# Expert blocks ordered by first token group, half of the final sums moved into the block loop, and smaller loads in the first attention layer

## The chip, the cores and the metric

The kernel runs as one program on one core of a Trainium2 chip. The metric is device time in microseconds (us) of one execution. The engines are named as the profile names them: PE (TensorE, with PEld for its weight loads), DVE (VectorE), ACT (ScalarE), POOL (GpSimd) and SP (SyncE); a "q" behind a name (SPq, POOLq) is the engine's instruction queue, from which DMAs are issued.

## The reference, cut to what matters

There are 32 batches of 112 rows with 256 features. Each of four branches normalises `x`, computes something and adds it to `x` under a gate:

```
x = x + tanh(g0) * attention_16_heads_of_16(norm(x), ctx)     # layer 0, 375 context rows per batch
x = x + tanh(g1) * gated_recurrence_over_32_batches(norm(x))
x = x + tanh(g2) * attention_16_heads_of_64(norm(x), ctx)     # layer 1
x = x + tanh(g3) * (shared_expert(norm(x)) + routed)          # 64 experts, 8 per row
aff = xf @ centroids.T;  idx = top_k(aff + bias, 8)
w = sigmoid(aff at idx), normalised over the 8
h = silu(xf @ W_up[e]);  routed[row] = sum over its 8 experts of w * (h @ W_down[e])
```

So 3584 rows go to 8 experts each, which makes 28672 pairs of a row and an expert.

## The kernel before

Layer 0 walks over 128 steps `n` (batch `b = n // 4`, four heads each). Keys come from PE and ACT, and eight small DMAs on the SP queue (L432, `kT<-k`) spread 16 heads over partitions; the queries of a group of four batches are spread by 16 more on the same queue (L416, `qp<-q`). `inputs(g)` (L359 to L368) loads `x`, the context and recurrence weights of a whole group from POOL's queue. PE, DVE and ACT follow the order as written; POOL does not, and is placed by the scheduler. Then come the recurrence and layer 1, in which `route(b)` picks the experts of batch `b` and, eight times per batch, POOL's indirect DMA (L286) scatters the 112 normalised rows with their weights into `xrows`, a table in HBM with a region for each expert. Rows stand there in order of batch.

The experts follow. Tables (L967 to L1032) are built from the counts per expert. The blocks of 128 rows come in two parts: the first 256 rows of each expert, as 64 steps `n < E` of two blocks, and then 136 single blocks, two a step, whose expert and place are found in the tables at run time. `run(lo, hi)` is the block loop; its PE, DVE, ACT and SP order is the written one. At step `n` it does, in this order:

- `rows_in(n+4)`: SP loads the rows of step n+4 (L1042; or, for `n >= E`, two register loads from `x_at`, L1048, and two DMAs, L1049). `xblk` has 5 buffers. Every eighth step up to 40, `weights` adds 2 MB of expert weights on SP.
- `turned(n)`: PE transposes (L1057), ACT copies (L1059), and DVE finds each row's weight and target (`own`, `dst32`, L1062 to L1072).
- `up(n-2)`: PE (L1085 or L1095), ACT (L1101), DVE (L1102).
- `down(n-4)`, or for `n >= E` `hidden_turned(n-4)` (L1109, L1111) and `down(n-6)`: PE (L1118), one half of `yblk` scaled by ACT (L1122) and the other by DVE (L1125), and two indirect DMAs by POOL (L1129) that scatter the two blocks into `yrows`, which has one place for each of the 28672 pairs. `yblk` has 4 buffers.

A second `run` for blocks past 136 stands under `tc.If(found > NSURE)`. At the end, 32 sums each load the 8 results of a batch's 112 rows, 896 KB, from `yrows` (L1176), add them up (L1179, L1180 on POOL, L1185), add the sum to `x` (L1186) and store each pair of batches (L1188).

Of the kernel before, what the change touches and what calls it, by code (L numbers as in the profile page):

```python
# [43 lines left out]
G = 4  # L44
# [8 lines left out]
SBLK = 2 * E  # L53
NSURE = 136
# [15 lines left out]
def flamingo_kernel(ctx: ExitStack, tc: tile.TileContext, a: dict, out: bass.AP):  # L70
# [34 lines left out]
    nc.vector.tensor_copy(e_col, e_col32)  # L105
    place32 = const.tile([S, TOPK], I32, tag="place32", name="place32")
    nc.gpsimd.iota(place32, [[1, TOPK]], base=0, channel_multiplier=B * TOPK)
# [4 lines left out]
    nc.vector.memset(seen[:, 0, :], 0.0)  # L112
    half = const.tile([S, G], F32, tag="half", name="half")
# [76 lines left out]
    def route(b, pool, psum):  # L190
# [16 lines left out]
            row[:, P_DST : P_DST + TOPK], place, float(b * TOPK), None, ALU.add  # L207
# [39 lines left out]
        po = psum.tile([S, D + E], F32, tag="mm", name=f"pos_{b}")  # L247

        pr = po[:, D:]
        nc.tensor.matmul(pr, earlier16, chosen, start=True, stop=False)  # L250
        nc.tensor.matmul(pr, ones16[:, :S], before, start=False, stop=True)
        nc.tensor.matmul(po[:, :D], hs, sdn, start=True, stop=True)
        nc.vector.reciprocal(w, w)
# [41 lines left out]
    with ExitStack() as att:  # L295
# [14 lines left out]
        with ExitStack() as ph:  # L310
# [48 lines left out]
            def inputs(g):  # L359
                nc.gpsimd.dma_start(  # L360
                    xs[g], a["x"][g * G : (g + 1) * G].rearrange("b s d -> s b d")
                )
                nc.gpsimd.dma_start(cts[g], a["ctxT"][:, g * G : (g + 1) * G, :])


                if 2 <= g < 6:
                    w, name = ((wg, "wg"), (ug, "ug"), (wot, "wot"), (uot, "uot"))[g - 2]
                    nc.gpsimd.dma_start(w, a[name].rearrange("(c p) m -> p c m", p=128))  # L368
# [35 lines left out]
            def queries0(g, i):  # L404

                pq = ps_m.tile([128, GT], F32, tag="mm", name=f"pq0_{g}_{i}")
                for k in range(2):
                    nc.tensor.matmul(
                        pq, wq[:, k, 128 * i : 128 * i + 128], xTs[g][:, k, :],
                        start=(k == 0), stop=(k == 1),  # L410
                    )

                q = kvp.tile([128, GT], F32, tag="q", name=f"q0_{g}_{i}")
                nc.scalar.activation(q, pq, AF.Identity, bias=bq4[:, i : i + 1], scale=0.25)
                for h in range(8):
                    nc.sync.dma_start(  # L416
                        qps[g % 2][h % 4 * 32 : h % 4 * 32 + 16, 2 * i + h // 4, :],
                        q[16 * h : 16 * h + 16, :],
                    )
# [120 lines left out]
            def output0(b):  # L540
# [10 lines left out]
                nc.tensor.engine, nc.vector.engine, nc.scalar.engine,  # L551
# [9 lines left out]
            for i in range(2):  # L561
                queries0(0, i)
# [3 lines left out]
            for n in range(4 * B + 7):  # L566
                b, g = n // 4, n % 4
                ng, turn = b // G + 1, (b % G, g)
                if ng < NG and turn == (0, 0):
                    inputs(ng)  # L570
# [27 lines left out]
                if ng < NG and turn in ((3, 1), (3, 2)):  # L598
                    queries0(ng, g - 1)
# [359 lines left out]

    w_at = wp.tile([1, NBLK], I32, tag="w_at", name="w_at")  # L960
    x_at = wp.tile([1, NBLK], I32, tag="x_at", name="x_at")
    n_blk = wp.tile([1, 1], I32, tag="n_blk", name="n_blk")
    first = wp.tile([128, SBLK + NBLK], F32, tag="first", name="first")
    nowhere = wp.tile([128, SBLK + NBLK], F32, tag="nowhere", name="nowhere")
    own = wp.tile([128, SBLK + NBLK, 2], F32, tag="own", name="own")
    dst32 = wp.tile([128, SBLK + NBLK], I32, tag="dst32", name="dst32")
    total = seen[:, B % G, :]  # L967
    with tc.tile_pool(name="tables", bufs=1) as ep:
        pc = ps_x.tile([E, 1], F32, tag="x", name="pc_n")
        nc.tensor.matmul(pc, total, ones16[:, 0:1], start=True, stop=True)  # L970
        n_e = ep.tile([E, 1], F32, tag="n_e", name="n_e")
        nc.vector.tensor_copy(n_e, pc)
# [6 lines left out]
        above = ep.tile([E, NT // 128 - 2], F32, tag="above", name="above")  # L979
        nc.vector.tensor_scalar(above, steps[:E, 2 : NT // 128], n_e, None, ALU.is_lt)  # L980
        blocks = ep.tile([E, 1], F32, tag="blocks", name="blocks")
        nc.vector.tensor_reduce(blocks, above, AX.X, ALU.add)
        pb = ps_x.tile([E, 1], F32, tag="x", name="pb_before")
        nc.tensor.matmul(pb, earlier[:E, :E], blocks, start=True, stop=True)
        pt = ps_x.tile([1, 1], F32, tag="x", name="pt_blocks")
        nc.tensor.matmul(pt, blocks, ones[:E, 0:1], start=True, stop=True)
        nc.vector.tensor_copy(n_blk, pt)
        before = ep.tile([E, 2], F32, tag="before", name="before")
        nc.vector.tensor_copy(before[:, 0:1], pb)
        nc.vector.tensor_tensor(before[:, 1:2], before[:, 0:1], blocks, ALU.add)  # L990

        nc.vector.tensor_scalar(before, before, 128.0, None, ALU.mult)
        is_e = ep.tile([E, NBLK], F32, tag="is_e", name="is_e")
        past = ep.tile([E, NBLK], F32, tag="past", name="past")
        nc.vector.tensor_scalar(is_e, steps[:E, :NBLK], before[:, 0:1], None, ALU.is_ge)
        nc.vector.tensor_scalar(past, steps[:E, :NBLK], before[:, 1:2], None, ALU.is_ge)
        nc.vector.tensor_tensor(is_e, is_e, past, ALU.subtract)
# [4 lines left out]
        nc.vector.tensor_copy(base[:, 2:3], before[:, 0:1])  # L1002
        nc.vector.tensor_copy(base[:, 3:4], n_e)
        of = []
        for i in range(4):
            wide = ep.tile([E, 128], F32, tag=f"wide{i}", name=f"wide_{i}")
            nc.vector.tensor_scalar(wide, ones[:E], base[:, i : i + 1], None, ALU.mult)
            pg = ps_x.tile([128, NBLK], F32, tag="x", name=f"pg_{i}")
            nc.tensor.matmul(pg, wide, is_e, start=True, stop=True)
            if i == 0:  # L1010
                nc.vector.tensor_copy(w_at, pg[0:1, :])
            else:
                t = ep.tile([128, NBLK], F32, tag=f"of{i}", name=f"of_{i}")
                nc.vector.tensor_copy(t, pg)
                of.append(t)
        region, start, n_of = of
        nc.vector.tensor_tensor(start, steps[:, 2:], start, ALU.subtract)
# [19 lines left out]
    live = {}  # L1037

    def rows_in(n):
        x = ep.tile([128, 2, PW], F32, tag="xblk", name=f"xblk_{n}", bufs=5)  # L1040
        if n < E:
            nc.sync.dma_start(  # L1042
                x, xrows[n * NT : n * NT + 256, :].rearrange("(i p) c -> p i c", p=128)
            )
        else:
            for i in range(2):
                e = 2 * n + i - SBLK
                at = nc.sync.value_load(x_at[0:1, e : e + 1], min_val=0, max_val=E * NT - 128)  # L1048
                nc.sync.dma_start(x[:, i, :], xrows[bass.ds(at, 128), :])  # L1049
        live[n] = [x]  # L1050

    def turned(n):
        x = live[n][0]
        px = ps_x.tile([128, 2, 2, 128], F32, tag="x", name=f"px_{n}")
        for i in range(2):
# [15 lines left out]
        nc.vector.tensor_reduce(own[:, 2 * n : 2 * n + 2, :], both, AX.X, ALU.add)  # L1071
        nc.vector.tensor_tensor(  # L1072
            dst32[:, 2 * n : 2 * n + 2], own[:, 2 * n : 2 * n + 2, 1],
            nowhere[:, 2 * n : 2 * n + 2], ALU.max,
        )
        live[n] = [xT]

# [36 lines left out]
    def down(n):  # L1114
        hT, ats = live.pop(n)
        py = ps_y.tile([128, 2, D], F32, tag="y", name=f"py_{n}")
        for i in range(2):
# [3 lines left out]
        y = ep.tile([128, 2, D], F32, tag="yblk", name=f"yblk_{n}", bufs=4)  # L1121
        nc.scalar.activation(  # L1122
            y[:, 0, :], py[:, 0, :], AF.Copy, scale=own[:, 2 * n, 0:1]
        )
        nc.vector.tensor_scalar(  # L1125
            y[:, 1, :], py[:, 1, :], own[:, 2 * n + 1, 0:1], None, ALU.mult
        )
        for i in range(2):
            disjoint("yrows", nc.gpsimd.indirect_dma_start(  # L1129
                out=yrows[:, :],  # L1130
                out_offset=bass.IndirectOffsetOnAxis(
                    ap=dst32[:, 2 * n + i : 2 * n + i + 1], axis=0
# [3 lines left out]
            ))  # L1136

    def run(lo, hi):
        with tc.manual_schedule(engines={
            nc.tensor.engine, nc.vector.engine, nc.scalar.engine, nc.sync.engine,  # L1140
        }):
            for n in range(lo, min(lo + 4, hi)):
                rows_in(n)
            for n in range(lo, hi + 6):
                if n + 4 < hi:
                    rows_in(n + 4)
# [11 lines left out]
                if lo <= n - 6 < hi and E <= n - 6:  # L1158
                    down(n - 6)

    sure = (SBLK + NSURE) // 2
    run(0, sure)
# [6 lines left out]
    ep = ctx.enter_context(tc.tile_pool(name="sum", bufs=4))  # L1169
    ys = {}  # L1170
    with tc.manual_schedule(engines={nc.vector.engine}):
        for b in range(B + 1):
            if b < B:

                y = ep.tile([S, TOPK, 2 * D], F32, tag="y8", name=f"y8_{b}")[:, :, :D]
                nc.sync.dma_start(  # L1176
                    y, yrows.rearrange("(p b k) d -> b p k d", b=B, k=TOPK)[b]
                )
                nc.vector.tensor_tensor(y[:, 0:4], y[:, 0:4], y[:, 4:8], ALU.add)  # L1179
                nc.gpsimd.tensor_tensor(y[:, 0:2], y[:, 0:2], y[:, 2:4], ALU.add)  # L1180
                ys[b] = y
            if b > 0:
                c = b - 1
                y, xb = ys.pop(c), xs[c // G][:, c % G, :]
                nc.vector.tensor_tensor(y[:, 0], y[:, 0], y[:, 1], ALU.add)  # L1185
                nc.vector.scalar_tensor_tensor(xb, y[:, 0], tg[:, 3:4], xb, ALU.mult, ALU.add)  # L1186
                if c % 2 == 1:
                    nc.scalar.dma_start(  # L1188
                        out[c - 1 : c + 1].rearrange("b s d -> s b d"),
                        xs[c // G][:, c % G - 1 : c % G + 1, :],  # L1190
                    )
# [57 lines left out]
```

## Time and profile before

| What | Value |
|---|---|
| Median of 6 runs | 2524.71 us (2517.46 to 2530.61) |
| Profiled execution, its own time | 2525.33 us |
| Its span, first to last instruction | 2523.5 us |
| Mean granted TensorE clock | 0.954 |
| PE busy, share of the span | 90% |
| DVE busy | 66% |
| POOL busy | 34% |
| Layer 0 / recurrence / layer 1 | about 27 to 580 / to 805 / 828 to 2015 us |
| Expert tables and blocks | about 2024 to 2396 us |
| Final sums | 2398.7 to 2523.5 us |

The page divides the span into 40 slices of 63 us and gives for each engine the busy share in tenths. A group of instructions is written "line engine operation out<-in xcount | busy us, mean ns of one | idle us of the engine before them <-what ended the idle time". In the timeline each row is start, duration, engine, line and operation, with the idle time before it in brackets. In the list of waits a row is "who waited <- for whom: us in total, times, longest".

### The profile page before, as it was taken

How to read it: one execution, taken by the hardware profiler on the slowest of the kernel's cores; microseconds unless marked ns; L12 is line 12 of the kernel's file. 1: busy time of each engine (PE TensorE's matmuls, PEld its weight loads, DVE VectorE, ACT ScalarE, POOL GpSimd, SP SyncE). 2: the span in 40 equal slices, each digit the busy share in tenths (PEclk: the TensorE clock that was granted, in tenths of full speed). 3: DMA queues.
4: the chain of work that ended last, by engine and by line, in shares of the span. 5: the costliest groups of instructions: out<-in, count | busy, mean ns of one | idle time of the engine just before them, and what ended most of it. 6: DMA issues, size and time to landing. Idle time of an engine off the chain costs nothing.

```text
span 2523.5 us, 55527 instructions
## 1 busy us (share of the span) xinstructions
PE 2278.0 (90%) x20058; PEld 1793.8 (71%) x20058; DVE 1672.1 (66%) x4933; ACT 1169.2 (46%) x3088; POOL 854.9 (34%) x1014
## 2 busy tenths in 40 slices
PE   6999999999998999999999999999999969999700
PEld 3777777777997777777777777777777657789600
DVE  4666666666335677777777777777777755577577
ACT  1555444443333555555555555555555435455300
POOL 4111111010000024343334334433333457777733
PEclk7999999999999999999999999999999979999955
DMA  8111111112800000000000000000000189876499
GB/s 232 31 31 30 29 29 31 31 30 88 268 1 1 1 5 29 29 29 27 27 29 28 28 27 29 29 29 29 25 29 29 39 294 314 249 200 197 122 274 250
DMA packets 142536, 203.87 MB, mean 81 GB/s; under 512 B 24983, under 2 KB 119785, under 8 KB 142256
## 3 DMA queue, kind: packets, MB, share of 16 engines
q1 hardware_dynamic: 104384, 103.25, 15.3%
q0 software_dynamic: 31536, 90.82, 10.8%
q10 hardware_dynamic: 6336, 6.16, 0.8%
q8 instruction: 164, 2.69, 0.5%
q14 instruction: 116, 0.95, 0.1%
HBM read 100.67 MB, written 88.74 MB: 75 GB/s over the span
## 4 chain that ended last, share of the span: by engine, by line
PE 52%; DMA 7%; DVE 4%; ACT 2%; issue 2%; POOL 1%; SPq 0%; POOLq 0%; ACTq 0%; DVEq 0%
PE ps_a L810 7%; PE pv L788 7%; PE pk L773 7%; PE pav L860 7%; PE po_a L875 5%; PE pt_a L839 5%; PE pq L760 4%; DMA y<-yrows 3%; PE py L1118 3%; DMA yrows<-yblk,dst 3%; PE ph L1095 2%; PE px L1057 1%; ACT kT L777 1%; DMA xblk<-xrows 1%; POOL yrows L1129 1%
## 5 line engine op out<-in xcount | busy, mean ns | idle before, releaser
L286 POOL DMA_INDIRECT xrows<-row,at x256 | 257.0, 1004 | 521.7 <-DVE at L283 329.1
L462 DVE TENSOR_REDUCE nm<-sc 112x1 f32<-112x375 f32 x512 | 258.3, 543 | 210.1 <-PE st L473 136.4
L815 ACT ACTIVATE p_a<-ps_a,nmax_a 112x375 f32<-112x375 f32 x512 | 286.6, 572 | 230.8 <-DVE nmax_a L814 230.8
L479 ACT ACTIVATE pT<-st 125x336 f32<-125x336 f32 x512 | 202.7, 448 | 276.4 <-PE st L473 276.4
L1129 POOL DMA_INDIRECT yrows<-yblk,dst x264 | 257.6, 976 | 97.7 <-issue 34.4
L839 PEld LDWEIGHTS pt_a<-ident,p_a 112*125 112x125 f32 x1536 | 224.5, 188 | 78.7 <-ACT v L795 19.2
L814 DVE TENSOR_REDUCE nmax_a<-ps_a 112x1 f32<-112x375 f32 x512 | 244.5, 540 | 29.6 <-PE ps_a L810 29.6
L458 PE MATMUL sc<-kT,qp 32*112 32x375 f32 x1024 | 247.8, 535 | 17.6 <-DMA kT<-k 11.8
L473 PE MATMUL st<-qa,kT 32*125 32x112 f32 x3072 | 238.1, 287 | 0.0
L839 PE MATMUL pt_a<-ident,p_a 112*125 112x112 f32 x1536 | 228.3, 271 | 0.6 <-ACT kT L777 0.6
L788 PE MATMUL pv<-wv,c 128*125 128x256 f32 x768 | 216.1, 390 | 10.4 <-ACT kT L777 6.5
L773 PE MATMUL pk<-c,wk 128*128 128x375 f32 x512 | 208.0, 488 | 4.2 <-ACT v L795 0.3
L860 PEld LDWEIGHTS pav<-pT_a,v 125*64 125x64 f32 x3072 | 148.0, 137 | 68.9 <-issue 52.2
L810 PE MATMUL ps_a<-kT,qT 64*112 64x375 f32 x1024 | 194.5, 498 | 0.0
L473 PEld LDWEIGHTS st<-qa,kT 32*125 32x125 f32 x3072 | 192.0, 187 | 3.2 <-DVE nm L462 0.4
L152 POOL TENSOR_SCALAR rstd<-stats 112x4 f32<-112x4 f32 x16 | 3.9, 246 | 553.7 <-DVE stats L147 553.4
L846 DVE COPY pT_a<-pt_a 125x448 f32<-125x448 f32 x128 | 78.9, 617 | 159.5 <-PE pt_a L839 159.5
L827 DVE TENSOR_SCALAR p_a<-p_a,inv_a 112x375 f32<-112x375 f32 x512 | 177.7, 411 | 4.5
L860 PE MATMUL pav<-pT_a,v 125*64 125x112 f32 x3072 | 175.5, 263 | 0.0
L777 ACT COPY kT<-pk 128x375 f32<-128x375 f32 x256 | 121.0, 473 | 115.4 <-PE pk L773 110.3
L788 PEld LDWEIGHTS pv<-wv,c 128*125 128x125 f32 x768 | 124.4, 188 | 29.4 <-ACT kT L777 21.5
L875 PE MATMUL po_a<-wo,oT 128*112 128x256 f32 x512 | 142.9, 402 | 0.0
(239 smaller groups left out, 4489.0 us busy)
## 6 DMA issues: line engine op xcount, KB each, us to landing
y<-yrows SPq DMA_DIRECT2D x32, 896.0 KB
xblk<-xrows SPq DMA_DIRECT2D x136, 140.0 KB
xrows<-blank POOLq DMA_DIRECT2D x2, 8960.0 KB
xblk<-xrows SPq DMA_DIRECT2D x64, 280.0 KB
kT<-k SPq DMA_DIRECT2D x512, 23.4 KB
wall<-in_w_up SPq DMA_DIRECT2D x7, 1024.0 KB
wall<-in_w_down SPq DMA_DIRECT2D x7, 1024.0 KB
c<-in_ctxT POOLq DMA_DIRECT2D x7, 750.0 KB
```

What stands on the lines that cost most here:

```text
L286: disjoint("xrows", nc.gpsimd.indirect_dma_start(out=xrows[:, :], out_offset=bass.IndirectOffsetOnAxis(ap=at[:, k : k + 1], axis=0), in_=r ...
L458: nc.tensor.matmul(sc, qps[b // G % 2][32 * j : 32 * j + 32, g, j0 : j0 + S], kTs[n % 6][32 * j : 32 * j + 32, :], start=True, stop=True,)
L462: nc.vector.tensor_reduce(nms[n % 3][:, j, 16:17], sc, AX.X, ALU.max, negate=True)
L473: nc.tensor.matmul(st[j][:, kc, :], kTs[m % 6][32 * j : 32 * j + 32, kc * KC : (kc + 1) * KC], qas[m][32 * j : 32 * j + 32, :], start=True ...
L773: nc.tensor.matmul(pk, wk[:, c * 128 : (c + 1) * 128], cts[b // G][:, b % G, :], start=True, stop=True,)
L788: nc.tensor.matmul(pv[:, i, :], ct[:, (lo + i) * KC : (lo + i + 1) * KC], wv[:, g * 256 : (g + 1) * 256], start=True, stop=True,)
L810: nc.tensor.matmul(sc, qT[r0 : r0 + 64, 2 * g + i, j0 : j0 + S], kT[r0 : r0 + 64, i, :], start=True, stop=True,)
L815: nc.scalar.activation(p[:, j, :], sc, AF.Exp, bias=nmax[:, j : j + 1], accum_out=tot[:, j : j + 1],)
L839: nc.tensor.transpose(pt[:, j * S : (j + 1) * S], p[:, j, kc * KC : (kc + 1) * KC], ident[:S, :S],)
L860: nc.tensor.matmul(po[64 * r : 64 * r + 64, i, :], v[:, kc, 64 * j : 64 * j + 64], pT[:, kc, j * S : (j + 1) * S], start=(kc == 0), stop=( ...
L875: nc.tensor.matmul(pos[b], outs[b][:, c, :], wo[:, c, :], start=(c == 0), stop=(c == 7))
L1129: disjoint("yrows", nc.gpsimd.indirect_dma_start(out=yrows[:, :], out_offset=bass.IndirectOffsetOnAxis(ap=dst32[:, 2 * n + i : 2 * n + i + ...
```

## The change

**Order of the blocks.** `route` counts, after each batch, how many rows each expert has (`counts`, one PE product and one DVE copy a batch). The tables sort the 136 later blocks by the batch of their first row instead of by expert. `yrows` is laid out batch, row, expert instead of row, batch, expert.

**Sums in the loop.** With the blocks in that order, all results of batch `b` are scattered once the first `8 * b` of the later blocks are done, if no more than that many have begun by then. `late` counts the batches below 16 for which this fails. If there is none, `run(0, sure, early=True)` is used, which from step 69 on does a quarter of a batch's sum in each step: SP loads two halves of 448 KB (in the first and second of four steps), DVE adds, ACT's queue stores. The load waits for all scatters issued before it; later scatters don't wait for it. Otherwise the plain `run(0, sure)` runs, and all sums stay at the end.

**Buffers.** `rows_in` runs 3 steps ahead instead of 4, `xblk` has 4 buffers and `yblk` 3. `own` and `dst` become small tiles of 10 buffers. For `n >= E` ACT scales both halves of `yblk`.

**Layer 0.** `inputs(n)` is called in every step and loads one batch's context, one batch's `x` or one half of a weight; POOL now follows the written order. The queries' spreading DMAs go to ACT's and SP's queue for the first group and to POOL's after that.

```diff
+    counts = const.tile([E, B], F32, tag="counts", name="counts")
...
+        if b > 0:
+            pn = po[:E, D + E :]
+            nc.tensor.matmul(pn, before, ones16[:, 0:1], start=True, stop=True)
+            nc.vector.tensor_copy(counts[:, b - 1 : b], pn)
...
-                if ng < NG and turn == (0, 0):
-                    inputs(ng)
+                inputs(n)
...
-                nc.tensor.engine, nc.vector.engine, nc.scalar.engine,
+                nc.tensor.engine, nc.vector.engine, nc.scalar.engine, nc.gpsimd.engine,
...
-                queries0(0, i)
+                queries0(0, i, (nc.scalar, nc.sync)[i])
...
-                    queries0(ng, g - 1)
+                    queries0(ng, g - 1, nc.gpsimd)
...
+        late = ep.tile([B, 1], F32, tag="late", name="late")
+        nc.vector.tensor_tensor(late, span[:, 1:2], planned, ALU.is_gt)
...
-        x = ep.tile([128, 2, PW], F32, tag="xblk", name=f"xblk_{n}", bufs=5)
+        x = ep.tile([128, 2, PW], F32, tag="xblk", name=f"xblk_{n}", bufs=4)
...
-        y = ep.tile([128, 2, D], F32, tag="yblk", name=f"yblk_{n}", bufs=4)
+        y = ep.tile([128, 2, D], F32, tag="yblk", name=f"yblk_{n}", bufs=3)
...
+            tc.declare_no_dep(
+                scatter.ins, group="sums", reason="these tokens have no more rows to come"
+            )
+            disjoint("yrows", scatter)
+
+    def early_sums(t):
+        b, k = t // 4, t % 4
+        def half(i):
+            if b < NEARLY:
+                y = ep.tile([S, 4, D + 8], F32, tag=f"y{i}", name=f"y{i}_{b}", bufs=1)[:, :, :D]
+                tc.add_to_no_dep_group("sums", results_in(b, y, 4 * i, 4).ins)
+                live["y", b, i] = y
+        def add(a, c):
+            nc.vector.tensor_tensor(a, a, c, ALU.add)
+        if k == 0:
+            half(1)
+            if 0 < b <= NEARLY:
+                y = live["y", b - 1, 0]
+                add(y[:, 0:2], y[:, 2:4])
+        if k == 1 and 0 < b <= NEARLY:
+            y, xb = live["y", b - 1, 0], xs[(b - 1) // G][:, (b - 1) % G, :]
+            add(y[:, 0], y[:, 1])
+            nc.vector.scalar_tensor_tensor(xb, y[:, 0], tg[:, 3:4], xb, ALU.mult, ALU.add)
+        if k == 1:
+            half(0)
+        if k == 2 and b % 2 == 0 and 0 < b <= NEARLY:
+            results_out(b - 2)
+        if k == 3 and b < NEARLY:
+            for i in range(0, 4, 2):
+                add(live["y", b, 0][:, i : i + 2], live["y", b, 1][:, i : i + 2])
...
-                if n + 4 < hi:
-                    rows_in(n + 4)
+                if n + 3 < hi:
+                    rows_in(n + 3)
...
+                if early and n >= E + EARLY:
+                    early_sums(n - E - EARLY)
...
-    run(0, sure)
+    is_late = nc.values_load(n_blk[0:1, 1:2], min_val=0, max_val=NEARLY)
+    with tc.If(is_late < 1):
+        run(0, sure, early=True)
+    with tc.If(is_late > 0):
+        run(0, sure)
     found = nc.values_load(n_blk[0:1, 0:1], min_val=0, max_val=NBLK)
     with tc.If(found > NSURE):
         run(sure, (SBLK + NBLK) // 2)
...
+    with tc.If(is_late > 0):
+        sums(0, NEARLY)
+    sums(NEARLY, B)
```

## The prediction

> **What bounds the kernel now.** I read the page's slices first, then the list of groups, then the waits, the chain and the timeline of each stage that the change touches.
>
> ```profile
> POOL 4111111010000024343334334433333457777733
> DMA  8111111112800000000000000000000189876499
> ...
> L1129 POOL DMA_INDIRECT yrows<-yblk,dst x264 | 257.6, 976 | 97.7 <-issue 34.4
> ```
>
> POOL is at 7 tenths only in the block loop. There are 264 scatters of 976 ns. The timeline of POOL in the later blocks shows what lies between them:
>
> ```profile
> 2219.99 0.98 POOL L1129 DMA_INDIRECT yrows<-yblk,dst  x1 [0.30 <-issue]
> 2221.26 0.97 POOL L1129 DMA_INDIRECT yrows<-yblk,dst  x1 [0.30 <-DVE both L1067]
> 2222.54 0.98 POOL L1129 DMA_INDIRECT yrows<-yblk,dst  x1 [0.30 <-issue]
> ```
>
> One starts every 1.28 us, and 264 x 1.28 = 338 us is the way from the first (2057.35) to the end of the last (2396.34). So POOL sets the block loop's time, 2.56 us a step, although the chain goes through PE there. PE needs 2.42 us a step and runs ahead until it is out of `yblk` buffers:
>
> ```profile
> ACT yblk L1122 <- DMA yrows<-yblk,dst: 86.2, 64, 4.1
> ```
>
> The final sums are bound by DMA at 269 GB/s, with DVE waiting for each load:
>
> ```profile
> L1179 DVE TENSOR_TENSOR y<-y x32: 1224/1225/1227, 2404.9 to 2516.2; 112x1024 f32<-112x1024 f32 x32
> ...
>   DMA y<-yrows: 36.7, 31
> ```
>
> That is (2516.2 - 2404.9) / 31 = 3.59 us a batch. In layer 0 PE is busy except where it waits for the small spreading DMAs, first from 20 to 65 us, where bulk loads fill the DMA engines (slice one: 8 tenths), then later:
>
> ```profile
> PE sc L458 <- DMA kT<-k: 5.5, 2, 3.5
> PE sc L458 <- DMA qp<-q: 5.5, 2, 5.3
> ...
> PE sc L458 <- DMA kT<-k: 6.3, 6, 1.5
> ```
>
> **The tail.** Sixteen sums leave it: 16 x 3.59 = -57.4 us. The condition decides whether they do. Counting the routes of the reference's own inputs, 17 later blocks have begun by batch 15 where 120 are allowed, none is late, and 129 of 136 are real. So the early sums run.
>
> **What they cost in the loop.** DVE gets about 2.8 us more per four steps (two adds of 512 elements and one more at half of L1179's 1.23, then 0.42 and 0.48) and loses four scalings of 0.48 to ACT; both have room. The new wait is what counts. The load of step n waits for the scatters of `down(n-6)`, issued in the same step, to land, and SP stands still meanwhile. Queued behind it on SP is `rows_in(n+4)`, for which PE's step n+4, and with it `down(n-2)`, waits. That is a loop from the landing of scatter n-6 to that of n-2, four steps:
>
> - SP issues the load: 0.33 us. Then two register loads and row DMAs; the pair's DMAs start 1.20 apart (1.53 for both, less 0.33), so the second starts 0.33 + 0.87 + 1.20 = 2.4 us after the landing.
> - The rows land 2.8 us later ("2210.90 2.82 DMA xblk<-xrows" in the chain): 5.2.
> - PE's step, transposes to the end of `py`: 3.2 us after a pause (2216.55 to 2219.72), 2.6 when it flows (2219.55 to 2222.13). I take 3.2: 8.4.
> - ACT's write to POOL's start: 0.75 (2056.60 to 2057.35): 9.2.
> - Two scatters: 1.28 + 0.98 = 2.26: 11.4.
> - Their landing: 1.6 to 2.3 us in the last steps (2380.98 to 2382.67, 2386.11 to 2388.37). With 2.0 the loop takes 13.4 us.
>
> Other traffic slows it: the 448 KB in front of the rows need half of 3.59, 1.8 us. Most is hidden under the 2.1 us in which SP prepares the row DMAs; I add 0.6. So 14.0 us, against 8 x 1.28 = 10.24 now. Sixteen batches, the last with no rows left to load: 15 x 3.76 = +56 us. Bounds: 12.4 (flowing PE, landing in 1.6) gives +32; 16 (rows 1 us later, and the 3.5 us that landings took between the weight bursts of the first 64 steps) gives +86.
>
> That SP stands still is in this trace already:
>
> ```profile
> SPq L1176 <- DMA yrows<-yblk,dst: 33.6, 1, 33.6
> ```
>
> SP reached the first final load 33.6 us early and issued nothing until the scatters had landed. [...]
>
> **Start of the loop.** Now five row loads go out before the 2 MB of weights (2042.87 to 2045.3), and PE waits at 2057.60 for the sixth, behind them. With four buffers the fifth is behind them, and step 4, which feeds POOL's first scatter, starts about 3 us later: +3 (0 to 5).
>
> **Three `yblk` buffers in steps below 64.** With three, POOL has four scatters, 5.1 us, to cover a landing and the 0.75 us to its start, so a landing over 4.4 us starves it. At each of six weight bursts landings took 5.6 to 6.1 us: about 1 us each, +5 (0 to 10).
>
> **Tables.** DVE waits 7.94 us for the first rows (2046.01), its tables done at 2038.1. The new ones add two passes over 832 elements (1.1 each by L280's 0.68 for 512), about 2 of small steps net, and three trips PE to DVE of 0.8: 6 us, hidden. Without that cover they would cost 6.
>
> **Skipped bodies.** One `If` is skipped now. Its cost shows as 3.3 us between SP's branch and its next instruction (2360.7 to 2364.0), 3.96 for PE's branch, and on POOL semaphores from the last scatter (2396.34) to the first load at 2398.70. Then there are three, one with 264 scatters in it. POOL's queue can run only some 5 us ahead of its last scatters: +6 (1 to 11).
>
> **Layer 1.** PE is 98% busy. 31 count products at 0.14 (L970, start to the next load of weights): +4.3 (0 to 7). The copies (0.15) lie in DVE's idle time.
>
> **Layer 0.** Without the bulk loads the first `kT` and `qp` should land without delay: of 11.0 us of waits some 6 go. PE's matmuls there take 0.83 where they later take 0.48, at a granted clock of 0.80 from 30 to 100 us; fewer pauses save perhaps 2. ACT gains eight issues of 0.4 to 0.6 ahead of the second query copy, which delays its DMAs. The later 6.3 us come when SP issues 16 `qp` DMAs between the `kT` ones; on POOL's queue, each 0.6 to 0.9 us, they have three steps of 3.9 us to land: -5. Together -13 (-20 to -4).
>
> [...]
>
> The new layout of `yrows` I cost at nothing: row blocks, which lie in one piece, are read at 140 KB in 0.585 us of DMA time (39.8% of 175 us over 119), 245 GB/s, no faster than `yrows` now.
>
> **Sum.** -57.4 + 56 + 3 + 5 + 6 + 4.3 - 13 = +4 us on the profiled 2525.33, which is 0.6 above the median: 2529, rounded to 2530. Ends of the terms other than the loop add to about -20 and +20.
>
> **Rivals.**
>
> *B, the wait doesn't bind.* If rows lead by enough, or PE's three loaded steps keep POOL fed, POOL keeps 2.56 us a step and the loop term is 0 to 10: 2525 - 57 + 5 + 5 = about 2478. For it: POOL has up to six scatters queued when a wait begins. Against: the loop above is longer than 10.24 in every variant that the rows allow.
>
> *C, the DMA engines decide.* Four steps need 4 x 1.6 us of DMA time now (62% of 175 us over 68 steps), and a sum adds 3.9 and its store 0.4: 10.7 of 14 us. If landings stretch at that load as in the first 64 steps, the loop takes 16: +86 instead of +56, 2559. It decides from a mean landing of scatters above 3.5 us.
>
> *D, the condition is false on the chip:* the plain loop and all sums at the end, 2525 + 3 + 5 + 4 + 10 - 13 = 2534. Against: the counts.
>
> **How the numbers follow.** Forecast (A) 0.58, B 0.15, C 0.22, D 0.05. A's own range is 2508 to 2552. To hold 8 in 10 the range reaches into B's upper part and over C: 2492 to 2565. A measurement of this kernel tells about 0.2%, 5 us, from no change. Faster: B 0.15 and a quarter of A, 0.30. Within: a quarter of A and some of D, 0.17. Slower: the rest of A, C and D, 0.53.
>
> **What would show it.** Right: POOL idle in later blocks of some 3 to 4 us every four steps, with SP waiting for `yrows` landings 30 times and PE waiting for `xblk`; first to last scatter about 400 us; a tail of 68 us; layer 0 shorter by about 13. Wrong: scatters still every 1.28 us from step 69 on (B), landings over 3.5 us (C), or 32 sums at the end (D). If PE never waits for rows, the loop I built the forecast on is not there.

## The result and the profile after

The kernel after takes 2551.56 us (median of 20 runs, 2544.46 to 2557.3), the kernel before beside it 2525.66 (46 runs): ratio 1.0098, interval [1.0083, 1.0113], 26 us slower. The forecast was 2530 in a range from 2492 to 2565, with slower as the likeliest outcome. The profiled execution of the kernel after took 2543.36 us with a span of 2541.6, so it lies 8 us under its median; the sums below are made on the spans, 2523.5 and 2541.6, which differ by 18.1.

First the slices of the page and the group of the scatters:

```profile
POOL 3333333201000033334334433333443466645543
PEclk8999999999999999999999999999999799988875
DMA  3122212116300000000000000000000588766639
...
L1201 POOL DMA_INDIRECT yrows<-yblk,dst x264 | 259.0, 981 | 198.4 <-ACT yblk L1189 129.3
```

The 264 scatters cost what they cost before (981 ns each), but POOL's idle time in front of them has doubled to 198.4 us, and it waits for ACT's `yblk` now. In the later blocks POOL falls from 7 tenths to 4 to 6, and the granted clock from full to 0.8. Below, the timeline of POOL in one batch of the loop (start, duration, and in brackets the idle time before it):

```profile
2289.54 0.97 POOL L1201 DMA_INDIRECT yrows<-yblk,dst  x1 [8.07 <-ACT yblk L1189]
...
2297.84 0.97 POOL L1201 DMA_INDIRECT yrows<-yblk,dst  x1 [0.30 <-ACT yblk L1197]
2299.12 0.97 POOL L1201 DMA_INDIRECT yrows<-yblk,dst  x1 [0.30 <-issue]
2304.79 0.97 POOL L1201 DMA_INDIRECT yrows<-yblk,dst  x1 [4.70 <-ACT yblk L1189]
```

The eight scatters start 1.28 us apart but for one gap of 0.93 us among the rows left out; then POOL has nothing to do for 4.7 us. SP's timeline of the same batch says why. The two loads of `y<-yrows` are the halves of the early sum:

```profile
2293.27 0.33 SPq L1271 DMA_DIRECT2D y<-yrows  x1
2294.45 2.08 SPq L1115 DMA_DIRECT2D xblk<-xrows  x2
2297.92 0.33 SPq L1271 DMA_DIRECT2D y<-yrows  x1
2299.10 5.97 SPq L1115 DMA_DIRECT2D xblk<-xrows  x6
2308.59 0.33 SPq L1271 DMA_DIRECT2D y<-yrows  x1
```

From one first half to the next it is 2308.59 - 2293.27 = 15.3 us. The six row DMAs are out at 2305.07; then SP stands still until the scatters have landed. The waits of the whole block loop (us, times, longest) add it up:

```profile
SPq L1271 <- DMA yrows<-yblk,dst: 98.7, 31, 7.1
...
PE px L1123 <- DMA xblk<-xrows: 44.6, 24, 4.0
...
POOL yrows L1201 <- ACT yblk L1189: 107.2, 42, 8.1
```

SP waits 31 times for landings, PE then for rows, POOL for PE's results. The tail is as wanted: half the sums, in this answer on the line of their first add,

```profile
L1290 DVE TENSOR_TENSOR y<-y x16: 1210/1225/1226, 2484.9 to 2533.9; 112x1024 f32<-112x1024 f32 x16
```

(2533.9 - 2484.9) / 15 = 3.27 us a batch. And in layer 0 PE's waits for the spreading DMAs have shrunk from 17.3 us to 2.7:

```profile
PE sc L481 <- DMA qp<-q: 1.9, 1, 1.9
PE sc L481 <- DMA kT<-k: 0.8, 2, 0.5
```

Stage by stage: the first row load is issued 26.9 us earlier than before; from there to the first scatter it takes 4.25 us more; from the first scatter to the end of the last 436.7 us in place of 339.0, +97.7; from there to the first final load 4.0 more; the tail 61 less. Sum: -26.9 + 4.25 + 97.7 + 4.0 - 61 = +18.

### The profile page after: what moved, and what is told of

Read it like the earlier page. It is cut to its first block, busy times and chain, and to the rows that moved or that the text cites. A ratio compares the mean times of both kernels' runs of the same rounds, so it can differ in the third digit from the quotient of the medians.

```text
span 2541.6 us, 56031 instructions
## 1 busy us (share of the span) xinstructions
PE 2315.9 (91%) x20103; PEld 1819.1 (72%) x20103; DVE 1643.6 (65%) x4937; ACT 1195.1 (47%) x3156; POOL 913.9 (36%) x1154
## 3 DMA queue, kind: packets, MB, share of 16 engines
q14 instruction: 127, 1.03, 0.1%
## 5 line engine op out<-in xcount | busy, mean ns | idle before, releaser
L1201 POOL DMA_INDIRECT yrows<-yblk,dst x264 | 259.0, 981 | 198.4 <-ACT yblk L1189 129.3
L836 DVE TENSOR_REDUCE nmax_a<-ps_a 112x1 f32<-112x375 f32 x512 | 244.4, 539 | 21.6 <-PE ps_a L832 18.1
L481 PE MATMUL sc<-kT,qp 32*112 32x375 f32 x1024 | 234.1, 527 | 2.7 <-DMA qp<-q 1.9
L1123 PE MATMUL px<-ident,xblk 128*128 128x128 f32 x528 | 91.9, 297 | 66.0 <-DMA xblk<-xrows 57.3
```

The costliest lines, as they stand in the source:

```text
L481: nc.tensor.matmul(sc, qps[b // G % 2][32 * j : 32 * j + 32, g, j0 : j0 + S], kTs[n % 6][32 * j : 32 * j + 32, :], start=True, stop=True,)
L836: nc.vector.tensor_reduce(nmax[:, j : j + 1], sc, AX.X, ALU.max, negate=True)
L1201: scatter = nc.gpsimd.indirect_dma_start(out=yrows[:, :], out_offset=bass.IndirectOffsetOnAxis(ap=dst[:, i : i + 1], axis=0), in_=y[:, i, ...
```

## The experiments

Two theories stood at the start. W: SP's wait for scatters that have only just been issued closes a loop through rows, PE, ACT and POOL, longer than POOL's 10.24 us a batch. C: the early loads crowd the DMA engines, and everything lands late. The edits are against the kernel after unless it says otherwise. Four of the kernels (`l0_only`, `plain_end`, `old_scatters`, `bufs34`) ran on a slower chip, on which the kernel before takes 2620 us, the other eight on one where it takes 2522, like the times above. So each is read against the kernel before beside it, by the ratio, and gains in us are worked out from the ratio.

**Older scatters.** `old_scatters`, and again on the other chip as `old_again`:

```diff
+SLACK = 4
-    nc.vector.tensor_copy(planned, planned32)
+    nc.vector.tensor_scalar(planned, planned32, -2.0 * SLACK, 0.0, ALU.add, ALU.max)
...
-                tc.add_to_no_dep_group("sums", results_in(b, y, 4 * i, 4).ins)
+                load = results_in(b, y, 4 * i, 4)
+                for m, s in scatters:      # (step, instruction) of all scatters so far
+                    if m >= E and m > E + EARLY + t - 6 - SLACK:
+                        tc.declare_no_dep(load.ins, s.ins, reason="later blocks")
+                tc.add_to_no_dep_group("sums", load.ins)
```

> The kernel after, with one edit: an early sum's load of step n no longer waits for the scatters of the last four steps, only for those of steps up to n-10, and the condition on the counts is stricter by the eight blocks that this leaves out. The same loads, bytes, adds and places in SP's queue; only the wait is on older scatters, which have landed. Theory W: the loop through SP, rows, PE, ACT, POOL and the landing is open; POOL goes back to 10.24 to 10.5 us per four steps, 15 x 5.2 = 78 us less: 2551.6 - 75 = about 2475. Theory C (the DMA engines are crowded by the loads of 448 KB): the period stays at 14 to 15.6 us, 2540 to 2551.

Measured on the slower chip: 2555.33 against 2620.47, ratio 0.9753 [0.9714, 0.9791]. For want of the kernel after beside it, that did not yet tell the theories apart. On the quicker chip the two ran together.

> The kernel after, unchanged, beside the next three on one chip. The first four kernels ran on a chip on which the kernel before takes 2620 us: there SP needs about 1.5 us for a register load and a row DMA (1.12 in the profile of before), so that SP's issuing, 3.3 us a step, sets the pace of the later blocks in place of POOL's 2.56. If this is such a chip, theory W gives the loop 15.6 us and about 1.5 more (two pairs of SP's and two of PE's register loads, 0.35 each): 17 a batch against 13.5 now, less the tail's 60, layer 0's 27, with 11 for the buffers: about the time of before, -20 to +10 us. On a chip like the first: +26 over before, as measured.

> The early loads wait for scatters four steps older (the same kernel as the run before with this edit), now beside the kernel after. Theory W: 45 us less than the kernel after where SP's issuing is slow, 75 us less where it is quick. Theory C (DMA engines crowded by the early loads): within 10 us of the kernel after.

The kernel after took 2546.68 against 2522.22, ratio 1.009 [1.0065, 1.0115], as at first. With the older scatters: 2489.02, ratio 0.9869 [0.9841, 0.9897], 58 us less than the kernel after and 33 less than before. The same loads are issued by the same engine at the same place. SP's timeline with the older scatters:

```profile
2270.20 0.33 SPq L1278 DMA_DIRECT2D y<-yrows  x1
2271.36 6.73 SPq L1116 DMA_DIRECT2D xblk<-xrows  x6
2278.19 0.39 SPq L1278 DMA_DIRECT2D y<-yrows  x1
2279.41 1.51 SPq L1116 DMA_DIRECT2D xblk<-xrows  x2
2281.81 0.33 SPq L1278 DMA_DIRECT2D y<-yrows  x1
```

The first half at 2278.19 follows the row DMAs at once, and one batch takes 2281.81 - 2270.20 = 11.6 us. SP's waits for landings between 2215 and 2460 us, first in the kernel after, then here, where the one that is left stands in front of the final sums:

```profile
SPq L1271 <- DMA yrows<-yblk,dst: 88.4, 29, 7.1
```

```profile
SPq L1278 <- DMA yrows<-yblk,dst: 7.3, 1, 7.3
```

So W holds and C falls as the cause: over 2235 to 2390 us this kernel moves 250 GB/s with a DMA share of 0.85, while the kernel after had only 0.66 in its loop. But the batch came down to 11.8 us on average, not to 10.24, hence 58 us and not 75.

**One step older.** `slack1` is the same with `SLACK = 1`.

> As that edit, but the loads wait for scatters one step older only. Theory W: the loop is as long as in the kernel after, but spans five steps in place of four, so a batch takes 4/5 of 15.6 us, 12.5: 47 us less than the kernel after where POOL sets the pace; where SP's issuing sets it (some 14 us a batch), one step of slack is about as good as four. A rival to W, that SP's standing still as such costs and not the way around: one step more changes little, under 15 us, since the scatters waited for have still not landed when SP comes to the load.

2489.32 us, ratio 0.9857 [0.9829, 0.9885]: as good as four steps, and 11.7 us a batch where I had 12.5. The rival, that standing still as such is what costs, falls. One step is enough: of SP's 29 waits for landings two are left, 13.6 us in all, the final sums' included, so scatters that are one step older have landed when SP comes to the load.

**The clock inside the loop.** In the kernel after, PE's step behind the pause is slow:

```profile
2298.31 0.41 PE L1123 MATMUL px<-ident,xblk 128*128 128x128 f32 x2 [1.60 <-DMA xblk<-xrows]
2298.91 0.44 PE L1123 MATMUL px<-ident,xblk 128*128 128x128 f32 x2 [0.19 <-DMA xblk<-xrows]
2299.69 0.71 PE L1161 MATMUL ph<-wall,xbT 128*128 x4 [0.34 <-issue]
2300.62 1.22 PE L1161 MATMUL ph<-wall,xbT 128*128 x4 [0.22 <-issue]
2301.63 0.63 PE L1175 MATMUL pv<-ident,h 128*128 128x128 f32 x2
2302.05 1.90 PE L1185 MATMUL py<-wall,hT 128*128 x4
```

`ph` starts with 0.71 us for four products and goes on with 1.22, and `py` takes 1.90 where it takes 1.03 in flow. The granted clock, third from the end of the row of this 1 us, is at half there:

```profile
2302.00:2303.00 1.00, 1.00 (x5) 0.82 (x4) 0.09 (x1) 0.26 (x1) 0.00 (x0) 0.50 0.90 288
```

In the trace's clock records of the loop it is at half once a batch, for 3.4 or 6.8 us. Two kernels fill the pause with idle transposes:

```diff
         px = ps_x.tile([128, 2, 2, 128], F32, tag="x", name=f"px_{n}")
+        if early and n >= E + EARLY + 4:
+            for _ in range((24, 8, 0, 0)[(n - E - EARLY) % 4]):
+                nc.tensor.transpose(px[:, 0, 0, :], ident, ident)
```

> The kernel after, with idle transposes of the identity (24 and 8 of them) queued on PE in front of the two steps of each batch whose rows come late, into the PSUM tile that the real transposes then fill. They fill most of PE's pause of 3 to 5 us and leave every wait as it is. PE's step behind the pause took 5.0 us in the kernel after, at a granted clock of 0.5, where I had 3.2. If the pause is what lowers the clock and the step lies in the loop: 1.5 us less a batch, 15 x 1.5 = 22 us less than the kernel after. Rival: the clock is lowered for another reason, or the step isn't in the loop: no gain, or up to 20 us more where the transposes run past the rows' landing.

2546.09 us, ratio 1.0094 [1.007, 1.0118]: no gain over the kernel after. The clock did come up, as these rows of 200 us of the loop show (length, PE, PEld, DVE, ACT and POOL busy, granted clock, DMA share, GB/s), first the kernel after in its second profile, then with the transposes:

```profile
2225.00:2425.00 200.00, 156.89 (x876) 128.68 (x875) 98.68 (x355) 84.16 (x195) 96.98 (x98) 0.86 0.64 190
```

```profile
2225.00:2425.00 200.00, 184.40 (x1335) 164.91 (x1334) 103.28 (x369) 88.60 (x204) 102.06 (x103) 0.98 0.66 195
```

Twelve batches of the timeline, averaged, tell where the gain went: from the last transposes of the rows to the end of `py` 2.98 us in place of 4.52, but from SP's first half to the first transpose of the rows 7.19 in place of 5.86. The idle transposes themselves stand in front of the rows, since PE, 92% busy now, is late from the steps before: in eleven of the twelve batches it does not wait for those rows at all.

> As the run with idle transposes, with fewer (14 and 4 in place of 24 and 8). With 24 the granted clock in the loop rose from 0.86 to 0.98 and PE's step behind the pause fell to 3.2 us, yet a batch still took 15.4 us, since the transposes ran past the landing of the rows by 0.5 to 1 us, and landings took longer. If that overrun ate the gain: with 14 (1.6 us) PE is free when the rows land, the clock stays above 0.9, and the time is 10 to 20 us under the kernel after's, ratio about 1.003. If the loop through the second load (which has no such pause) decides: as the kernel after, ratio 1.009.

(14 and 4 in place of 24 and 8.) 2546.82 us, ratio 1.0111 [1.0082, 1.014]. Now the pause sits in front of the second step of the batch, whose rows come after the second half: its way from transposes to `py` takes 4.33 us, that of the first step 2.86, and the batch 15.9 as before. So two such ways run side by side in each batch, one behind each half, and the slow step now sits in the other one. What the slow clock costs by itself stays open: the filler takes the place of what it saves.

**What remains of the loop.** `act_loads` is the kernel with older scatters, and ACT issues the early loads:

```diff
-                load = results_in(b, y, 4 * i, 4)
+                load = results_in(b, y, 4 * i, 4, nc.scalar)
```

> The kernel with loads that wait for scatters four steps older, and one more edit: ACT issues these loads in place of SP. With the older scatters the profile still has 22 to 25.6 us per 16 scatters in the later blocks in place of 20.5, and SP needs 12 us a batch there to issue (6 row DMAs in 7.2 us, two more and two early loads in the rest). Reading: SP's issuing is then the longest of the engines' work. If so, SP has eight row DMAs of 1.12 left, 9 us, POOL's 10.24 decides again, and the time falls by another 15 to 25 us, to about 0.98 of before. Rival: what is left comes from landings (three buffers for yblk, rows behind 448 KB), then no change; or ACT, which is needed for the scalings, stands behind the loads' waits: 10 to 30 us more.

2485.76 us, ratio 0.9862 [0.9826, 0.9898], the same, and 11.7 us a batch. My reading that SP's issuing sets what is left falls. The waits from 2220 to 2400 us:

```profile
DVE y L1231 <- DMA y<-yrows: 37.4, 15, 4.0
ACT xbT L1126 <- DVE both L1134: 37.2, 21, 3.4
...
ACT yblk L1190 <- DMA yrows<-yblk,dst: 23.3, 16, 2.7
```

Now ACT stands behind the load in place of SP, for DVE: the two tiles of the early sums have one buffer each, and a load waits until DVE has added the batch before (the list names `both`, a DVE instruction just behind that add). With the load on SP, SP waited for the same DVE instruction, 23.1 us in 13 waits from 2225 to 2395 us. Those waits, the `yblk` landings with three buffers, or a DMA share of 0.85 may each hold the remaining 1.5 us a batch. Taking one of them away was not tried, so which one it is stays open.

**The buffers.** `bufs34` is the kernel before with three `yblk`, four `xblk` and rows three steps ahead.

> The kernel before, with the change's buffers alone: three yblk instead of four, four xblk instead of five, rows three steps ahead instead of four. If the gaps of POOL in the first 64 steps of the kernel after (11.2 us in all) and its later start (4.25 us) come from the buffers: 2525.7 + 15 = 2540. Rival: they come from the early sums or the new order, and POOL's queue covers a landing as before: 2525.7 + 3 = 2529.

2633.02 us against 2620.47, ratio 1.0049 [1.0023, 1.0075], +13 us, as expected from the parts. But on this chip the trace places some 7 us of it in front of the first scatter, not in the gaps of the first 64 steps: the way from the first transposes to the first scatter is 16.5 us (9.2 in `l0_only`, which ran beside it with the old buffers), the way over all scatters 435 and 436. The gaps are better read on the quicker chip: over the first 128 scatters, kernels with three buffers (after twice, `old_again`, `slack1`, `warm`, `warm14`) lose 9 to 12 us against 1.28 a scatter, those with four (before, `l0_loads`, `l0_queues`) 1.4 to 4.9.

**No early sums.** `plain_end` has the conditional bodies and the early sums left out; its 32 sums stand at the end.

```diff
-    with tc.If(is_late < 1):
-        run(0, sure, early=True)
-    with tc.If(is_late > 0):
-        run(0, sure)
+    run(0, sure)
...
-    with tc.If(is_late > 0):
-        sums(0, NEARLY)
-    sums(NEARLY, B)
+    sums(0, B)
```

> The kernel after, with the early sums left out: one plain block loop, and all 32 sums at the end; blocks still in the new order, three buffers for yblk, the new layer 0. Theory W (SP's wait for scatters that have just been issued closes a loop of 15.6 us a batch): the loop is back at 1.28 us between scatters from step 64 on, the tail is 125 us. By what the traces give for each part: 2525.7 - 28 (layer 0) + 4 (counts in layer 1) + 4 (start of the loop) + 11 (three buffers in the first 64 steps) = 2517, and up to 2527 if the exit of the conditional bodies costs less without it. Rival: the new order or the buffers cost POOL its gaps also without early sums; then the loop stays longer by over 50 us and the time is 2570 to 2600.

2606.68 us, ratio 0.996 [0.9927, 0.9994], -10 us (-19 to -2 by the interval): just below the expected -9 to +1 against before, with which the interval overlaps, and far from the rival's +45. Order, counts, tables and buffers together cost some 17 us beside layer 0's gain of 27. That the loop returns to 1.28 us a scatter is not shown by this run: on this chip 16 later scatters take 25.5 to 27.9 us here and 26.2 to 30.4 in `l0_only`, where the quicker chip has 20.5.

**Layer 0.** `l0_only` is the kernel before with all of the change's layer 0, `l0_loads` with the small loads alone, `l0_queues` with the queries' queues alone.

> The kernel before, with the change's layer 0 alone: small loads spread over the steps, the first queries issued by ACT and SP, the later ones by POOL. The marks of layer 0's steps in the kernel after are 28.2 us earlier at the last step than in the kernel before (11.1 of them by step 4, the rest in jumps at the group boundaries). If that is all of it and nothing behind layer 0 gives it back: 2525.7 - 28 = 2497. Rival: the later jumps belong to something else in the kernel after; then only the start is won, 2525.7 - 11 = 2514. My prediction's own term, -13, would give 2513.

> The kernel before with the small loads of layer 0 alone, in POOL's written order; the queries stay on SP. Both parts together gave the ratio 0.9898. My prediction had -8 for this part and -5 for the queries' queues. By the step marks 11 us are won by step 4 and 17 in jumps at the group boundaries, where SP's 16 query DMAs stood in front of the kT loads. If the jumps belong to the queues: 11 to 13 us less, last step mark 13 us earlier than in the kernel before. Rival: the bulk loads caused the jumps as well; then the whole 27.

> The kernel before with the queries' queues of layer 0 alone: the first copy on ACT and SP, the later ones on POOL; bulk loads as before. If the queues are what the later jumps come from: about 15 us less (17 in the jumps, less what the bulk loads, in front of the queries on POOL's queue, delay). My prediction's term was -5. Rival: the queries on POOL's queue stand behind bulk loads and the spreading of rows, and arrive late: no gain, or 5 to 10 us more.

`l0_only`: 2597.67 against 2620.47, ratio 0.9898 [0.985, 0.9945], -27 us by the ratio. `l0_loads`: 2518.14, 0.9981 [0.995, 1.0012]; `l0_queues`: 2511.64, 0.9959 [0.994, 0.9979]. The last step mark of layer 0 (`pm`, 607.4 us in the kernel before, whose layer 0 ends at about 616 us and not at the 580 of the table ahead) leaves out what differs behind layer 0: 580.8, 599.4 and 591.3. So the loads give 8.0 us, the queues 16.1, and both 26.6. With the loads alone 12.2 us are won by step 4, and 4.2 of them are lost again later. In the kernel with the queues alone PE is never idle from 65 to 265 us and the clock stays full:

```profile
65.00:265.00 200.00, 200.00 (x3011) 155.08 (x3009) 135.81 (x370) 102.43 (x258) 52.85 (x82) 1.00 0.13 32
```

In the kernel before, six waits for `kT` at group boundaries took 6.3 us in layer 0 behind the start. What follows one of them is more than the wait. First the wait itself, then the windows of 1 us behind it (the clock is the third number from the end):

```profile
403.91 1.23 PE L458 MATMUL sc<-kT,qp 32*112 32x375 f32 x3 [1.46 <-DMA kT<-k]
```

```profile
404.00:405.00 1.00, 1.00 (x10) 0.57 (x12) 0.20 (x1) 0.00 (x0) 0.00 (x0) 1.00 0.11 29
405.00:406.00 1.00, 1.00 (x29) 0.89 (x29) 0.85 (x3) 0.34 (x1) 0.00 (x0) 0.86 0.25 63
406.00:407.00 1.00, 1.00 (x21) 0.47 (x11) 0.71 (x3) 0.46 (x2) 0.00 (x0) 0.50 0.11 26
...
412.00:413.00 1.00, 1.00 (x32) 0.79 (x26) 0.52 (x2) 0.30 (x1) 0.00 (x0) 0.73 0.13 33
413.00:414.00 1.00, 1.00 (x25) 0.74 (x15) 0.85 (x4) 0.49 (x2) 0.00 (x0) 1.00 0.18 45
```

The clock is halved from 406 to 412 us: 0.14 + 6 x 0.5 + 0.27 = 3.4 us are lost behind a wait of 1.46. Together 4.9, and the step marks of the kernels before and after part by 5.1 us there. Not every wait has this price: of the six, only this one and one of 1.52 us, at 331.5, are followed by a slow clock (3.4 us at half from 334.03); behind 1.10 and 1.38 us, and two waits under 0.5, it stayed full.

## Why the prediction was right, and which of its terms were off

The direction was right, and for the reason given: SP's wait, in front of the rows that the same scatters need later on, closes a loop longer than POOL's pace. The traces carry the chain as predicted (POOL idle once a batch, SP 31 waits, PE waiting for `xblk`), and letting the load wait for older scatters, with its place, issuer and bytes as they were, turned 1.009 into 0.987. While SP waited for landings it issued nothing (98.7 us in 31 waits); in this kernel that cost 58 us, by `old_again`.

*The loop* was mis-sized. It stood at 14.0 us a batch and +56 in all; the trace has +88 (97.7 less 9.6 by which the first 64 steps grew), 82 of it as 15 batches of 15.7 us in place of 10.24. Its links, averaged over twelve batches of the first profile after, and in brackets of the second: rows on PE 6.5 us behind the load (6.25) where I had 5.2 and 0.6 for traffic; PE's step 3.65 (4.52) where I had 3.2; to POOL's start 0.99 (0.93) for 0.75; two scatters 2.39 (2.39) for 2.26; the landing 1.98 (1.91) for 2.0. Sum 15.5 (16.0). Links of this kind fill the batch whatever bounds it; that they form a loop is shown by `old_again`. Two terms were mainly too small: the way of the rows to PE, by 0.7 us (0.45), and PE's step, by 0.45 (1.3). For the step I took a place where PE had paused for 1.05 us and the clock had stayed full (1.00 from 2208 to 2222 us in the kernel before); in the loop the pause is up to 4.0 us and the clock goes to half behind it. I had also priced one way only. In the first profile PE pauses in front of the rows behind the first half in five of the twelve batches, and in front of those behind the second half in the other seven. The whole lies just above the upper bound that I had given, +86.

*Rival C* gave 2559, nearer the number than the forecast, but by another mechanism: it needed DMA engines that are short. They were 0.66 busy in the loop, and with more traffic in less time the older scatters won 58 us. Its point of decision, a mean landing above 3.5 us, told nothing: the median from issue to landing was 4.2 us in the first profile after and 3.0 in the second, with a batch no shorter, and SP goes on 2.0 us after the end of POOL's last instruction in both. Rivals B and D fell: the wait binds, and the profile has 16 sums at the end.

*Layer 0* was -28 where I had -13. The loads gave 8.0 for 6 + 2, by luck: 12.2 won at the start less 4.2 lost later. The queues gave 16.1 for 5: I counted the later waits, 6.3 us, at less than their own length and left out the half clock behind two of them, 10.2 us, which costs another 5.1. That makes 11.4 of the 17 us in the later jumps of the step marks; the rest is not accounted for.

*The rest:* three `yblk` buffers 9.6 for 5 (11.0 us lost in the first 64 steps against 1.28 a scatter, where the kernel before loses 1.4), at the end of the range of 0 to 10; the start 4.25 for 3; layer 1 3.8 for 4.3; the way out of the bodies 4.0 for 6; the tail -61 for -57.4, with 3.27 us a batch for 3.59; the tables hidden, DVE's idle time in front of the rows going from 7.94 to 3.48 us. On the spans the sum is +18 where I had +4: the loop's +32 and the buffers' +5 outweigh layer 0's -15 and the smaller gains. That the misses of the loop and of layer 0 have opposite signs is luck, and the sum looked better than its parts by it. Both hold a slow clock behind pauses that I had left out, but how much of the loop's miss it makes is not shown. The other 8 us to the median are the profiled execution's.

A version beats both kernels: with the load waiting for scatters that are one step older (`slack1`), or four (`old_again`), the change is worth 1.4%, 1.3%, of the time before.

## What to carry to other kernels

When a transfer is moved into a loop, look first at what its issuing queue must wait for and what is queued behind it: here the things behind fed the thing that was waited for, and the loop's length, 15.7 us a batch, not POOL's 10.24, was the new pace. The cure was to wait for older work: one step was enough (`slack1`, 0.9857 where the kernel after has 1.009). And look at the granted clock behind a pause of PE: behind 1.46 us it fell to half, and 3.4 us more were lost; behind 1.38 us it stayed full.

## What the runs showed of the hardware that was not expected

**Behind some short pauses PE's clock fell to half, later and for longer.** 1.46 us without a product at 402.45 to 403.91 us, full clock for 1.8 us, then half for 6.8 (from the shares in the rows above). The length of the pause alone does not tell: 1.52 us before 331.5 us was followed by 3.4 us at half, 1.38 us before 259.65 by none, and in `l0_loads` 1.54 us before 254.84 by none and 1.44 us before 327.22 by 3.4 us. In the clock records of the kernel before (layer 0 behind 61 us) and of the kernel after (its loop), every stretch at half clock is 3.41 or 6.83 us long, and the full ones between them are whole multiples of 3.41 us. Filling the pause in the loop held a mean of 0.95 (`warm14`) and 0.98 (`warm`) where the kernel after has 0.86.

**On one chip a queue pauses between its instructions.** On the slower chip twelve row DMAs, with a register load between each two, took SP 17.43 us, 1.55 from one to the next (timeline of `l0_only`):

```profile
2280.94 17.43 SPq L1058 DMA_DIRECT2D xblk<-xrows  x12
```

In the kernel before, on its chip, eighteen took 20.10, 1.16 from one to the next:

```profile
2279.77 20.10 SPq L1049 DMA_DIRECT2D xblk<-xrows  x18
```

Neither the register load nor the DMA instruction is slower as such: their medians are 0.27 and 0.33 us in `l0_only` as in the kernel before. But now and then an instruction of the queue takes 0.7 us, even one that only checks a register (0.018 us by its median). Here are that one's shortest, median and longest time in ns from 2220 to 2350 us, in the same kernel on the slower chip (`old_scatters`) and on the quicker one (`old_again`):

```profile
L1115 SPq SEQ_ASSERT  x71: 3/18/715, 2221.5 to 2347.1; - x71
```

```profile
L1115 SPq SEQ_ASSERT  x87: 18/18/18, 2220.2 to 2349.1; - x87
```

What holds the queue up is not shown. On the slower chip the later blocks run at 26 to 30 us per 16 scatters in place of 20.5 (`l0_only`), PE waits between its products of one step where it reads a register (18.0 us in 51 waits from 2210 to 2350 us, 2.8 in 10 before), and the kernel before takes 95 us more. Layer 0 takes about the same on both: the change's last step mark stands at 580.8 us in `l0_only`, at 579.2 in the kernel after. In the later blocks SP's issuing, not POOL, may set the pace of the plain loop there; no run tests it. It is not the whole: the first 64 steps, in which SP reads no register for the rows, are slower too, 12.4 us per 8 scatters in most of them in place of 10.2.
